# The last pair's second products one slot later, and the residual sum of an attention and expert kernel on VectorE

## The chip, the cores and the metric

The kernel runs on one core of one Trainium2 chip. The time is that of the device in microseconds (us), a median over runs; a profile of one execution lies beside it.

## The reference

The input x has 8 sequences of 512 rows of 256 floats. All of it is fp32, and the output has the shape of the input. `ln` is a layer norm over a row, without weights.

```python
x = x + ln(attn(ln(x)))          # 16 heads of 128 in 4 groups, causal; bias and position added to q and k
x = x + ln(moe(ln(x)))           # all rows as one batch

def attn(x):
    q = (x @ wq + bq) + pe ; k = (x @ wk + bk) + pe ; v = x @ wv + bv     # k, v: 4 groups of 4 heads
    return (softmax(causal(q @ k.T / sqrt(128))) @ v) @ wo

def moe(x):
    # softmax over 64 experts, best 6 of each row, at most 64 rows for an expert;
    # silu(x @ w_gate) * (x @ w_up) @ w_down for each, plus a shared expert of the same form
    ...
```

Note that `ln` does not change when a number is added to a whole row.

## The kernel before

**Slots.** The loop `for k in range(NK)` (line 1450) runs over 128 units: 8 sequences times 16 slots; a slot is one pair of row tiles and one group of heads. `b, s = divmod(k, NH)` are the sequence and the slot in it. The order of instructions on all engines is the order in which the loop's body calls its helpers (a manual schedule), so each engine has one queue, in that order. In each slot the unit k gets its scores (`scores`, psc on TensorE, reduced by VectorE, exponentials on ScalarE) and its weighing (`weigh`, reciprocal on VectorE, four TENSOR_SCALARs on GpSimd). In the next slot `turned` transposes 32x32 blocks on VectorE, sends them out to DRAM (`ex_d`, four DMAs on SyncE's queue) and reads them back as `et`. One slot later `mix` multiplies et by v (pav on TensorE, line 639), and ScalarE moves the result to `ao`.

**The projection in pairs.** For sequences 1 to 5 (`CROSSED`), the product with wo is done for two units at a time, a pair j. It has two parts. `straight` makes three products of ao (tile ps, bank o0), in the even slot. `cross` has GpSimd form four sums of ao (tile crossed), and `across` multiplies these (tile pc, bank o1). `add_up(j, 0)` and `add_up(j, 1)` add the banks to `partial`. For pairs 0 to 6 of a sequence, `across` and `add_up(j, 1)` stand in the odd slot. The last pair, n = 7, is due in slots 2 and 3 of the following sequence; before the change both of its parts stand in slot 2. `combine(b, 1)` on GpSimd then makes half of the rows o of the projection from partial (six instructions, lines 744 to 749).

**The feed-forward steps.** While sequence b + 1 runs, `feed_forward(b)` gives steps for sequence b, to be run at a place of a slot: `A` behind the weighing, `B` behind the projection's products, `M` behind the queries of later units, `D` at the slot's end. The steps that matter here, before the change:

| place | step | what it does |
|---|---|---|
| 2D | `copies` | combine(b, 1) |
| 3M | `scales(o)` | VectorE: statistics of o; GpSimd: rs_o, a power of -0.5 |
| 4A | `residual_sums` | normalizes o (sequences 1 to 4: VectorE makes shift_o, ScalarE does four ACTIVATEs; sequence 5: VectorE, four TENSOR_SCALARs), then GpSimd adds it to the rows xt, four TENSOR_TENSORs |
| 5M | `scales(xt)` | statistics of the new rows, rs_f on GpSimd |
| 5B | `store` | GpSimd's queue: DMA of xt, 512 KB, to x1_d |
| 6A | `rows` | normalizes the rows into xg (VectorE, and half of them ScalarE for sequences up to 4) |
| 6M | `turn` | VectorE transposes xg (into the buffer that o had), SyncE sends it out and reads it back (`exr_d`) |

**Buffers and queues.** The rows x of a sequence are in one of two buffers. The rows of the sequence after next are loaded by SyncE in slot 6 (`load_x`, line 187), behind that slot's et and once the store of x1 has read the buffer; their statistics (`st_a`) are taken by VectorE in slot 7. The tiles psc and third take turns in three PSUM banks, which VectorE frees.

Of the kernel before, what the change touches and what calls it, by code (L numbers as in the profile page):

```python
# [16 lines left out]
ALU = mybir.AluOpType  # L17
# [3 lines left out]
B, T, E = 8, 512, 256  # L21
NT = B * T
NI = T // P
# [21 lines left out]
CROSSED = range(1, EARLY + 1)  # L45

@with_exitstack
def sandwich_kernel(ctx, tc, x, wq, bq_t, wkv, bk_t, bv, wo, gate_wt, w_gate, w_up, w_down,
                    sh_gate_t, sh_up_t, sh_down_t, pe_t, out):
    nc = tc.nc  # L50
# [32 lines left out]
    def norm_scales(tiles, name, order=range(NI)):  # L83

        n = len(tiles)
        st = small.tile([P, n, 6], F32, tag="st", name=f"st_{name}")
        for i in order:
            nc.vector.bn_stats(st[:, i, :], tiles[i])
        return scales_of(st, n, name)
# [11 lines left out]
    def shifts(mv, rs, name):  # L101

        shift = small.tile([P, NI], F32, tag="shift", name=f"shift_{name}")
        nc.vector.scalar_tensor_tensor(shift, mv[:, :, 0], -1.0, rs, ALU.mult, ALU.mult)
        return shift

    def scale_on_act(dst, src, rs, shift, i):
        nc.scalar.activation(dst, src, AF.Identity, bias=shift[:, i : i + 1], scale=rs[:, i : i + 1])

    def tiles_of(t):  # L110
        return [t[:, i, :] for i in range(NI)]

    def rows_of(d, first):
        return d[first : first + T, :].rearrange("(i p) e -> p i e", p=P)

    def normalize(dst, src, mv, rs, i):
        nc.vector.tensor_scalar(dst, src, mv[:, i, 0:1], rs[:, i : i + 1], ALU.subtract, ALU.mult)

    def on_act(dst, src):
        nc.scalar.copy(dst, src)  # L120
# [35 lines left out]
    with ExitStack() as part:  # L156
# [497 lines left out]
        def tiles_at(j):  # L654

            return (1, 2) if j % 2 else (0, 3)

        def project(j, i):
            b, n = divmod(j, 2 * G)
            if n == 0 and i == 0:  # L660
                po[b] = [ps_o.tile([P, 2, E], F32, tag=f"o{n}", name=f"po_{b}_{n}") for n in range(2)]
            ao = results[j][:, tiles_at(j).index(i)]
            for h in range(QPG):
                nc.tensor.matmul(po[b][i // 2][:, i % 2, :], lhsT=ao[:, h, :], rhs=whole[j // 2][h],
                                 start=n == 0 and h == 0, stop=n // 2 == G - 1 and h == QPG - 1, skip_group_check=True)
# [46 lines left out]
        def multiply(j, factors, name, tag):  # L712
            bank_ = ps_o.tile([P, len(factors[0]), P], F32, tag=tag, name=f"{name}_{j}")
            for pair in range(2):
                for n, (a, w) in enumerate(factors[pair]):
                    nc.tensor.matmul(bank_[:, n, :], lhsT=a, rhs=w, start=pair == 0 and n == 0,  # L716
                                     stop=pair == 1 and n == len(factors[0]) - 1, skip_group_check=True)
            return bank_

        def straight(j):  # L720
            x11, x12, _, x22 = sides_of_results(j)
            w = sets[j // 2, 0]
            po[j, 0] = multiply(j, [[(x[:, n], w[k][:, n]) for k, x in enumerate((x11, x12, x22))] for n in range(2)],
                                "ps", "o0")

        def across(j):
            w, t = sets[j // 2, 1], crossed.pop(j)
            po[j, 1] = multiply(j, [[(t[:, k, n], w[k][:, n]) for k in range(4)] for n in range(2)], "pc", "o1")

        def add_up(j, part):  # L730
            b, n = divmod(j, 2 * G)
            sums, bank_ = partial[:, n % 2, (0, 3)[part] : (3, 7)[part], :], po.pop((j, part))
            if n < 2:
                on_act(sums, bank_)
            else:
                nc.vector.tensor_add(sums, bank_, sums)

        def combine(b, odd):

            t = partial[:, odd]  # L740
            if not odd:
                outs[b] = p1.tile([P, NI, E], F32, tag="xn", name=f"o_{b}")
            first, second = [outs[b][:, i, :].rearrange("p (u e) -> p u e", u=2) for i in tiles_at(odd)]
            nc.gpsimd.tensor_add(first[:, 0], t[:, 0], t[:, 1])
            nc.gpsimd.tensor_add(t[:, 5], t[:, 0], t[:, 5])
            nc.gpsimd.tensor_add(t[:, 6], t[:, 5], t[:, 6])
            nc.gpsimd.tensor_add(t[:, 3], t[:, 4], t[:, 3])
            nc.gpsimd.tensor_add(second, t[:, 2:5:2], t[:, 6:7].to_broadcast([P, 2, P]))
            nc.gpsimd.tensor_add(first[:, 1], t[:, 5], t[:, 3])

        def projected(k):

            j, odd = divmod(k, 2)
            j -= 2
            b, n = divmod(j, 2 * G)
            return j, odd, b, n, n == 2 * G - 1

        def projections(k):

            j, odd, b, n, last = projected(k)  # L760
            if j < 0:
                return
            if b not in CROSSED:
                for i in (() if odd else tiles_at(j)) if last else tiles_at(j)[odd : odd + 1]:
                    project(j, i)
            elif not odd:
                straight(j)
            elif not last:
                across(j)

        def projections_before(k):
# [4 lines left out]
        def projections_behind(k):  # L776
            j, odd, b, n, last = projected(k)
            if b in CROSSED:
                if not odd:
                    add_up(j, 0)  # L780
                elif not last:
                    add_up(j, 1)
                if last and not odd:
                    across(j)

        def projections_end(k):
            j, odd, b, n, last = projected(k)
            if b in CROSSED:
                if last and not odd:
                    add_up(j, 1)  # L790
                if n == 2 * G - 2 and odd:
                    combine(b, 0)

# [196 lines left out]
        def gate_up_hidden(key):  # L990
            l = pairs[key]
            pgu = l.pop("pgu")
            nc.vector.scalar_tensor_tensor(l["hid"], l["hid"], 1.0, pgu[:, 0, :], ALU.add, ALU.mult)
            nc.vector.scalar_tensor_tensor(l["hid"], l["hid"], 0.5, pgu[:, 1, :], ALU.mult, ALU.mult)
# [195 lines left out]
        def feed_forward(b):  # L1190


            xt, sums = seqs[b]["x"], po.pop(b, None)
            l = {}
# [10 lines left out]
            def scales(src, name):  # L1205
                l["scales"] = norm_scales(tiles_of(src), f"{name}{b}")

            def residual_sums():
# [7 lines left out]
                for i in range(NI):  # L1216
                    nc.gpsimd.tensor_add(xt[:, i, :], xt[:, i, :], l["o"][:, i, :])

            def store():
                nc.gpsimd.dma_start(out=rows_of(x1_d, b * T), in_=xt)  # L1220

            def rows():
                mv, rs = l.pop("scales")
                l["xg"] = p1.tile([P, NI, ROW], F32, tag="xg", name=f"xg_{b}")
                shift = shifts(mv, rs, f"f{b}") if b < EARLY else None
                for i in range(NI):
                    if b < EARLY and i % 2:
                        scale_on_act(l["xg"][:, i, :E], xt[:, i, :], rs, shift, i)
                    else:
                        normalize(l["xg"][:, i, :E], xt[:, i, :], mv, rs, i)  # L1230

            def turn():
                if b < EARLY - 1:
# [15 lines left out]
            def go(which, n=1):  # L1249
                return lambda: [next(l[which]) for _ in range(n)]  # L1250

            steps = {
                "2D": copies, "3M": lambda: scales(l["o"], "o"), "4A": residual_sums,
                "5M": lambda: scales(xt, "f"), "5B": store, "6A": rows,
                "6M": turn, "7A": shared_gate, "7B": go("f"), "8A": gate,
                "8D": go("r"), "9D": go("r"),
            }
            def choice_behind(steps):
                choose, then = steps.pop("8D"), steps.get("9A", lambda: None)
                return steps | {"9A": lambda: (choose(), then())}  # L1260

            if b == B - 2:
                steps["6D"] = steps.pop("6M")
            if b < B - 2:
                steps |= {"9A": go("f"), "9B": go("f"), "11A": go("f"), "11B": go("f")}
            if b < EARLY:
# [8 lines left out]
                steps = choice_behind(steps)  # L1275
# [15 lines left out]
            def down_late():  # L1291
# [3 lines left out]
            steps = choice_behind(steps) | {  # L1295
                "10A": go("r"), "10B": mark, "10D": gather_rows, "11D": lambda: gate_up("late"),
                "12A": lambda: gate_up_hidden("late"), "12D": lambda: turn_hidden("late"), "13A": down_late,
            }
# [151 lines left out]
        for k in range(NK):  # L1450
            b, s = divmod(k, NH)
# [86 lines left out]
            if s == 2 and b:  # L1538
                behind = feed_forward(b - 1)
# [34 lines left out]
        with tc.For_i(0, table["rest"], 1) as n:  # L1574
# [5 lines left out]
            for b in range(EARLY, B):  # L1580
                q, tag = [(p1, "hid"), (wpool, "e0"), (wpool, "e1")][b - EARLY]
                xg = q.tile([P, NI, LROW], F32, tag=tag, name=f"rest_xg_{b}")
# [75 lines left out]
```

## Time and profile before

| | us |
|---|---|
| median of three runs | 1350.15 (1346.76 to 1351.22) |
| the profiled execution | 1346.28 |
| its span, first to last instruction | 1344.6 |
| TensorE busy | 1319.8 |
| VectorE, GpSimd, ScalarE busy | 911.5, 660.3, 546.8 |

The granted clock of TensorE was 0.997 of full speed. The profile names engines PE (TensorE; PEld is its load of weights), DVE (VectorE), ACT (ScalarE), POOL (GpSimd), SP (SyncE); a q behind one is its queue. A group's row gives the source line, engine, operation, tiles written and read, shapes and count, then busy us, mean ns of one, idle time before it and what ended that. A timeline's row has the start, the time from first start to last end, the engine and line, and in brackets the idle time before it with what ended it. A row of the waits gives who waited for whom, us in total, times and the longest. A row of a tile gives the shortest, median and longest duration in ns. A row of windows has for each stretch the busy us of PE, PEld, DVE, ACT and POOL, the clock, the share of the 16 DMA engines and GB/s. An fp32 matmul is two records.

### The profile page before, as it was taken

The numbers are of one execution on the slowest core, as the hardware profiler recorded it, in microseconds if no ns is written. First come the engines' busy times: TensorE is split into PE (matmuls) and PEld (weight loads), VectorE is DVE, ScalarE is ACT, GpSimd is POOL, SyncE is SP. The second block draws the span as 40 slices with busy tenths as digits, with TensorE's granted clock in tenths as the row PEclk, the third lists the DMA queues.
The fourth block names the chain that finished last, engine by engine and source line by source line (L and its number), as shares of the span: only waits on it lengthen the run. The fifth ranks groups of instructions, "written<-read, shape, count | busy, mean of one in ns | idle before, by whom it ended". The sixth has DMA issues, their size and how long they took to land. (4 is left out here: it accounts for less than half of the span.)

```text
span 1344.6 us, 21778 instructions
## 1 busy us (share of the span) xinstructions
PE 1319.8 (98%) x6746; PEld 1018.7 (76%) x6746; DVE 911.5 (68%) x2931; ACT 546.8 (41%) x1665; POOL 660.3 (49%) x1080
## 2 busy tenths in 40 slices
PE   9999999999999999999999999999999999999997
PEld 7877887888778887788778877876667676767774
DVE  5575577777887678777886778666656444567645
ACT  3333354334443454344433443434343334444523
POOL 4556463436452563446434643355545444477711
PEclk9999999999999999999999999999999999999999
DMA  8676677756775676566765667579999889777712
GB/s 268 176 219 208 201 215 219 205 185 211 220 218 174 201 226 213 177 209 204 224 193 162 204 189 202 171 213 303 307 284 281 246 239 299 182 239 262 234 36 72
DMA packets 160435, 285.53 MB, mean 212 GB/s; under 512 B 17292, under 2 KB 123437, under 8 KB 160317
## 3 DMA queue, kind: packets, MB, share of 16 engines
q1 hardware_dynamic: 122893, 212.14, 52.6%
q0 software_dynamic: 13328, 36.05, 9.1%
q10 hardware_dynamic: 24096, 35.92, 8.5%
q8 instruction: 55, 0.90, 0.3%
q14 instruction: 63, 0.52, 0.1%
HBM read 168.44 MB, written 115.61 MB: 211 GB/s over the span
## 5 line engine op out<-in xcount | busy, mean ns | idle before, releaser
L584 POOL TENSOR_SCALAR e<-e,recip 128x512 f32<-128x512 f32 (+1 forms) x504 | 245.3, 525 | 424.1 <-DVE recip L580 367.7
L574 ACT ACTIVATE e<-e,least 128x32 f32<-128x32 f32 (+1 forms) x504 | 258.5, 514 | 260.4 <-DVE least L570 235.1
L639 PE MATMUL pav<-et,v 128*128 128x256 f32 x1280 | 300.4, 382 | 11.5 <-DMA et<-ex_d 8.9
L639 PEld LDWEIGHTS pav<-et,v 128*128 128x128 f32 x1280 | 241.5, 191 | 52.8 <-issue 7.1
L566 PE MATMUL psc<-kt,qt 128*128 128x32 f32 (+15 forms) x1024 | 274.9, 407 | 0.9 <-DVE qt L431 0.4
L570 DVE CUSTOM_DVE_ANT_0 e<-psc,mask 128x32 f32<-128x32 f32 (+1 forms) x504 | 204.2, 430 | 96.4 <-PE psc L566 93.8
L650 ACT ACTIVATE ao<-pav,bv_sb 128x256 f32<-128x256 f32 x255 | 107.1, 471 | 368.5 <-PE pav L639 344.7
L566 PEld LDWEIGHTS psc<-kt,qt 128*128 128x128 f32 x1024 | 161.5, 191 | 59.4 <-issue 25.9
L602 DVE STREAM_TRANSPOSE eb<-e 128x1024 f32<-128x1024 f32 (+1 forms) x252 | 197.5, 822 | 2.0 <-POOL e L584 1.5
L1021 POOL DMA_INDIRECT y_d<-dd,idx x32 | 51.1, 1597 | 93.2 <-ACT e L574 27.2
L574 ACT ACTIVATION_READ_ACCUMULATOR e<-e,least 128x1 f32 x504 | 94.6, 188 | 0.0
L716 PEld LDWEIGHTS pc<-set,crossed 128*128 128x128 f32 x640 | 77.0, 192 | 4.9 <-issue 1.7
L716 PE MATMUL pc<-set,crossed 128*128 128x128 f32 x640 | 78.8, 276 | 0.6 <-POOL crossed L710 0.6
L426 PE MATMUL pq<-xnt,wq_sb 128*128 128x256 f32 x320 | 75.5, 380 | 0.0
L716 PEld LDWEIGHTS ps<-set,ao 128*128 128x128 f32 x480 | 59.9, 192 | 15.3 <-issue 7.4
L470 PE MATMUL pq_back<-rows_joined,heads 128*128 128x256 f32 x264 | 71.3, 379 | 0.0
L388 PEld LDWEIGHTS pv<-wkv_sb,xnt 128*128 128x128 f32 x512 | 65.9, 192 | 4.5 <-issue 1.1
L388 PE MATMUL pv<-wkv_sb,xnt 128*128 128x128 f32 x512 | 67.5, 275 | 0.5 <-ACT ao L650 0.5
L426 PEld LDWEIGHTS pq<-xnt,wq_sb 128*128 128x128 f32 x320 | 59.2, 190 | 9.2 <-issue 0.7
L379 DVE SCALAR_TENSOR_TENSOR kt<-pk,bk_sb,pe_sb 128x512 f32<-128x512 f32 x32 | 24.0, 750 | 60.5 <-PE pk L377 58.5
L470 PEld LDWEIGHTS pq_back<-rows_joined,heads 128*128 128x128 f32 x264 | 50.2, 190 | 16.2 <-issue 8.2
L377 PE MATMUL pk<-xnt,wkv_sb 128*128 128x512 f32 x128 | 60.2, 593 | 0.3 <-ACT xnt L120 0.3
(281 smaller groups left out, 2017.6 us busy)
## 6 DMA issues: line engine op xcount, KB each, us to landing
ex_d<-eb SPq DMA_DIRECT2D x504, 160.0 KB
et<-ex_d SPq DMA_DIRECT2D x126, 640.0 KB
wgu<-in_w_gate ACTq DMA_DIRECT2D x32, 352.0 KB
wgu<-in_w_up ACTq DMA_DIRECT2D x32, 352.0 KB
wd<-in_w_down ACTq DMA_DIRECT2D x32, 352.0 KB
set<-wc_d SPq DMA_DIRECT2D x20, 512.0 KB
set<-ws_d SPq DMA_DIRECT2D x20, 384.0 KB
y<-y_d POOLq DMA_DIRECT2D x10, 512.0 KB, 6.8
```

The costliest lines, as they stand in the source:

```text
L377: nc.tensor.matmul(pk, lhsT=wkv_sb[:, c, g, 0, :], rhs=s["xnt"][:, c, :], start=c == 0, stop=c == NC - 1)
L388: nc.tensor.matmul(pv[:, i, :], lhsT=s["xnt"][:, c, ts(2 * n + i, P)], rhs=wkv_sb[:, c, g, 1, :], start=c == 0, stop=c == NC - 1, skip_gro ...
L426: nc.tensor.matmul(pq[:, n, :, :], lhsT=wq_sb[g][:, c, ts(2 * pair + n, D)], rhs=seqs[b]["xnt"][:, c, :].rearrange("p (u v) -> p u v", v=P ...
L470: nc.tensor.matmul(out, lhsT=factor[0], rhs=factor[1], start=first, stop=last, skip_group_check=True)
L566: nc.tensor.matmul(psc[:, :w], lhsT=halves[k // 2][:, at, :, :].rearrange("d h t -> d (h t)"), rhs=seqs[b]["kt"][g][:, :w], start=True, st ...
L570: nc.vector.tensor_tensor_reduce(out=e, in0=psc[:, :w].rearrange("p (c t) -> p c t", t=BS), in1=mask[:, T - w :].rearrange("p (c t) -> p c ...
L574: nc.scalar.activation(e, e, AF.Exp, bias=l["least"][:, q : q + 1], scale=-1.0, accum_out=l["total"][:, q : q + 1])
L584: engine.tensor_scalar(e, e, recip[:, q : q + 1], 1.0, ALU.mult, ALU.mult)
L602: nc.vector.transpose(eb[:, :, first : first + count, :, :].rearrange("p a j r t -> p j a r t"), weighed[k % 2][:, end - count : end, :, : ...
L639: nc.tensor.matmul(pav[n // NI][:, :, n % 2, :], lhsT=seqs[b]["v"][g][:, j, :], rhs=et[:, :, first + j, :], start=j == 0, stop=j == count ...
L650: nc.scalar.activation(ao, pav[n // NI][:, :, n % 2, :], AF.Identity, bias=bias)
L716: nc.tensor.matmul(bank_[:, n, :], lhsT=a, rhs=w, start=pair == 0 and n == 0, stop=pair == 1 and n == len(factors[0]) - 1, skip_group_chec ...
```

## The change

The last pair of a crossed sequence loses its exceptions: its `across` and `add_up(j, 1)` go to slot 3, as with all other pairs. For sequences 1 to 5 the steps behind are moved: combine to 3D, the statistics of o to 4A, the residual sum to 5A, the store to 5D. The sum is now made by VectorE in one instruction for each tile, o = o * rs + xt. This lacks -mean * rs, a number for each row (shift_o). The norm of the rows is taken from o as it is. The shift is added by GpSimd, xt = o + shift_o, just before the store, four TENSOR_SCALARs in place of four TENSOR_TENSORs.

```diff
             elif not odd:
                 straight(j)
-            elif not last:
+            else:
                 across(j)
...
                 if not odd:
                     add_up(j, 0)
-                elif not last:
+                else:
                     add_up(j, 1)
-                if last and not odd:
-                    across(j)
...
             if b in CROSSED:
-                if last and not odd:
-                    add_up(j, 1)
                 if n == 2 * G - 2 and odd:
                     combine(b, 0)
...
+            def residual_products():
+                mv, rs = l.pop("scales")
+                l["shift_o"] = shifts(mv, rs, f"o{b}")
+                for i in range(NI):
+                    nc.vector.scalar_tensor_tensor(l["o"][:, i, :], l["o"][:, i, :], rs[:, i : i + 1], xt[:, i, :],
+                                                   ALU.mult, ALU.add)
+
+            def shifted_store():
+                for i in range(NI):
+                    nc.gpsimd.tensor_scalar(xt[:, i, :], l["o"][:, i, :], l["shift_o"][:, i : i + 1], 1.0, ALU.add, ALU.mult)
+                store()
...
+                src = l["o"] if "shift_o" in l else xt
                 for i in range(NI):
                     if b < EARLY and i % 2:
-                        scale_on_act(l["xg"][:, i, :E], xt[:, i, :], rs, shift, i)
+                        scale_on_act(l["xg"][:, i, :E], src[:, i, :], rs, shift, i)
                     else:
-                        normalize(l["xg"][:, i, :E], xt[:, i, :], mv, rs, i)
+                        normalize(l["xg"][:, i, :E], src[:, i, :], mv, rs, i)
...
+            if b in CROSSED:
+                steps.pop("4A"), steps.pop("5B")
+                steps |= {"3D": steps.pop("2D"), "4A": steps.pop("3M"), "5A": residual_products,
+                          "5M": lambda: scales(l["o"], "f"), "5D": shifted_store}
```

## The prediction

> **What bounds the kernel now.** I read the page first, then TensorE's list of waits, then the timelines of TensorE, SyncE, VectorE and GpSimd around slots 4 to 8 of sequence 3, where the steps of sequence 2 run, and the DMA share by windows there. "Sequence 3, slot 4" is the slot that starts with the first psc of that unit (470.70 us; slots 5, 6, 7, 8 start at 478.72, 487.58, 495.69, 503.65).
>
> ```profile
> PE 1319.8 (98%) x6746; PEld 1018.7 (76%) x6746; DVE 911.5 (68%) x2931; ACT 546.8 (41%) x1665; POOL 660.3 (49%) x1080
> ...
> PE pav L639 <- DMA et<-ex_d: 8.9, 8, 2.8
> PE pav L639 <- DVE shift_o L104: 1.3, 3, 0.4
> PE pc L716 <- POOL crossed L710: 0.6, 1, 0.6
> ```
>
> TensorE is busy 98%: of 1344.6 us only 24.8 are idle, head and tail among them. The change takes no matmul away, so it can only remove waits, or make new ones. Waits near it are the last two rows and part of the first.
>
> ```profile
> 476.49 2.40 PE L639 MATMUL pav<-et,v 128*128 128x256 f32 x10 [0.45 <-DVE shift_o L104]
> ...
> 471.85 0.34 SPq L612 DMA_DIRECT2D et<-ex_d  x1
> ...
> 490.56 1.86 SPq L606 DMA_DIRECT2D ex_d<-eb  x4
> 494.91 0.34 SPq L612 DMA_DIRECT2D et<-ex_d  x1
> 495.41 0.40 SPq L187 DMA_DIRECT2D x<-in_x  x1
> ...
> 500.17 2.32 PE L639 MATMUL pav<-et,v 128*128 128x256 f32 x10
> ```
>
> The first row is the wait of slot 4. It is put down to VectorE's shift_o, but I take it for the transfer of et: that was issued 4.64 us earlier, and the same wait in sequences 2, 4 and 5 ends 4.50, 4.65 and 4.40 us after its et. So pav needs about 4.65 us from the issue of et. In slot 7 it has 5.26 us (500.17 - 494.91): 0.61 us to spare. SyncE's queue is in order: that et waits for the landing of ex_d, and the load of x stands behind it.
>
> ```profile
> 483.87 1.40 DVE L88 BATCH_NORM_STATS2 st_f<-x 128x6 f32<-128x256 f32 x4
> 485.19 0.36 DVE L94 BATCH_NORM_AGGREGATE mv_f<-st_f 128x2 f32<-128x6 f32 x4
> 485.58 0.40 DVE L96 TENSOR_SCALAR ve_f<-mv_f 128x4 f32<-128x4 f32 x1
> 487.78 0.75 DVE L379 SCALAR_TENSOR_TENSOR kt<-pk,bk_sb,pe_sb 128x512 f32<-128x512 f32 x1 [1.79 <-PE pk L377]
> ...
> 501.30 1.41 DVE L88 BATCH_NORM_STATS2 st_a<-x 128x6 f32<-128x256 f32 x4 [0.91 <-DMA x<-in_x]
> ...
> 485.21 0.81 POOL L1220 DMA_DIRECT2D x_d<-x  x1
> 486.08 1.03 POOL L98 TENSOR_TENSOR rs_f<-ve_f,mhalf 128x4 f32<-128x4 f32 x1
> ```
>
> In slot 5 VectorE has 1.79 us idle before kt; from kt to the end of slot 6 it has next to none. GpSimd issues the store of the sums before rs_f. In slot 7 VectorE already waits 0.91 us for x.
>
> **Part by part.** *Second products to slot 3.* 16 matmul records (1.79 us of TensorE's order) leave slot 2 and enter slot 3: same work, two slots of about 8 us in place of 9.90 and 6.18. Slot 3 being longer, TensorE reaches slot 4's pav 1.8 us later after the transposes that feed et. Gain: the waits of sequences 2 to 5, 0.29 + 0.45 + 0.44 + 0.14 = 1.32 us. If another cause stood behind shift_o it would be 0. In slot 3, pav of the unit before comes 1.8 us later in its slot, and its slot starts as much earlier: no change. In sequence 6 the products wait 0.61 us for GpSimd's crossed; half a turn later that is made: -0.61 us, or 0 if the slot waits elsewhere.
>
> *Steps half a slot later.* combine is six GpSimd instructions of about 3 us behind slot 3's weighing; they end some 1.7 us into slot 4, before VectorE's reciprocal there (476.28 - 470.70 = 5.6 us in), behind which 4A's statistics (1.4 + 0.36 + 0.17 = 1.9 us) now stand. VectorE was idle 2.22 us at the end of slot 4, so they fit; queued behind them is only ask_sum, whose reader is in slot 5. Cost 0. The add_up of part 1 moves too: 0.68 us of VectorE in slot 3, where the statistics of o leave 1.9.
>
> *Sum by VectorE.* ScalarE loses 4 x 0.586 us for blocks 1 to 4 and GpSimd 4 x 0.728 us, neither on TensorE's path: 0. VectorE gains, in slot 5, shift_o (0.09) and four products of 128x256 with two SBUF inputs. The nearest rows:
>
> ```profile
> L1399 DVE SCALAR_TENSOR_TENSOR x<-y,rs_y,x x4: 480/480/485, 1339.8 to 1340.9; 128x256 f32<-128x256 f32 x4
> ...
> L117 DVE TENSOR_SCALAR o<-o,mv_o,rs_o x8: 381/575/801, 924.8 to 1176.7; 128x256 f32<-128x256 f32 x8
> ```
>
> L1399 is the same form with GpSimd idle, one each 0.40 us. Four of L117 beside GpSimd's weighing took 2.09 us (0.52 each; alone their median on x is 0.40). The new four run beside slot 5's weighing. At 0.40 they need 1.69 us of the 1.79: hidden, with 0.10 left. I take 0.50, nearer to the row with the same neighbour: 2.09 us, 0.30 over. What is late then is kt, and behind it the reductions of slot 6. The eight psc matmuls took 2.16 us in slot 6 and 2.00 in slot 7, so they already follow VectorE there; I let the 0.30 through in four sequences: +1.2 us (0 at 0.40; 6.0 at 0.80).
>
> By the Trainium skill, "GPSIMD Engine Reference", section "Key points", GpSimd shares its SBUF interfaces with VectorE and contends with instructions that have two SBUF inputs. That speaks against the change: this trace has no such pair, L117 being the other kind that the page names. Were the page wrong for these, the term would be 0 and the sum 1.2 us less.
>
> *Shift at the store.* rs_f now waits for VectorE until about 487.7 (485.98 + 1.7) where it began at 486.08. Behind it on GpSimd: four TENSOR_SCALARs (0.467 apart as L1338, 1.9 us), the store's issue (0.81), four crossed (2.9) and slot 6's weighing. So: rs_f to 488.8, store issued at 490.7 in place of 485.21, crossed done at 494.4, weighing from there (before: 493.31) to 496.4. Its reader is slot 7's transpose at 497.05, and ScalarE's next ao needs crossed's inputs free by 495.1: both just hold, cost 0. The store is another matter.
>
> ```profile
> 487.00:488.00 1.00, 1.00 (x5) 0.61 (x4) 0.22 (x1) 0.00 (x0) 0.92 (x3) 1.00 1.09 352
> ...
> 491.00:492.00 1.00, 1.00 (x7) 0.87 (x6) 0.85 (x4) 1.00 (x3) 0.00 (x0) 1.00 0.62 125
> 492.00:493.00 1.00, 1.00 (x6) 0.90 (x5) 1.00 (x3) 0.27 (x2) 0.00 (x0) 1.00 0.96 182
> ```
>
> Before, it had the DMA engines to itself (352 GB/s, last columns DMA share and GB/s). Issued at 490.7 it starts some 1.4 us later, amid ex_d, which holds them at a share of 0.96. 512 KB at 352 GB/s is 1.5 us; by so much ex_d lands later, hence et, x and what follows on SyncE. Bounds: 0 if it slips between, 2.9 at the 182 GB/s of ex_d. I take 1.5. Slot 7's pav has 0.61 to spare: +0.88 each in sequences 2, 3 and 4, +2.6 us (0 to 6.9). Sequence 5's slots 6 and 7 are longer (8.99 and 12.16) and cover it. x lands 1.5 later; VectorE's tail of slot 7, which ended 503.58, ends 505.07, and slot 8 starts 0.88 later, at 504.53: the first reduction comes 0.54 into it in place of 0.43, +0.1 each, +0.3 (0 to 4). The store itself lands in about 4 us, before SyncE reaches x.
>
> *Sum*: -1.32 - 0.61 + 1.2 + 2.6 + 0.3 = +2.2 us. The profiled execution took 1346.28 (span 1344.6), 3.9 under the median of the three runs, so 1348.5 there; from the median 1350.15, **1352.3**.
>
> **Rivals.** *Quiet case*: store and products hidden, only the first two terms act: -1.9, 1348.2. For: DMA is free from 494.5 to 496. Against: the share of 0.96 where the store goes.
>
> *Slower*: VectorE overruns slot 5. At 0.80 per product (the longest L117) the overrun is 4 x 0.80 + 0.09 - 1.79 = 1.5 us, 6.0 over four sequences in place of 1.2: +7.0, 1357.2. It decides from 0.61 per product on, where the whole sum passes +4. For: the 0.10 us left in slot 5. Against: other instructions with an SBUF and a PSUM input keep 0.48 beside the weighing.
>
> *Faster*: nothing is added, and in sequence 6 the waits for et in slots 4 and 5 (1.80 and 1.00) go as slot 3 grows: -1.9 - 2.8 = -4.7, 1345.4. Against: these transfers queue behind weight loads, which the change doesn't touch.
>
> **How the numbers follow.** Forecast 0.33, with its own range 1350 to 1354; quiet 0.15; slower 0.35; faster 0.15; 0.02 left. About 0.3% (4 us) is what can be told from no change here; the three runs spread 4.5. Forecast and quiet lie within it: 0.48. Faster 0.16 with a little of what is left, slower 0.36. The range leaves out a tenth at each end: 1345.5 to 1358.
>
> **What would show it.** Right: slots 2 and 3 near 8 us; no wait at pav in slot 4; a new wait for et at slot 7's pav of 0.5 to 1.3 us in sequences 2 to 4, its et issued about 1.5 later; the four products at 0.4 to 0.6 apart. Wrong: products at 0.8, kt late by a microsecond; or no wait in slot 7; or SyncE standing at the load of x for the store.

## The result, and the profile after

Over eight runs each, measured side by side, the changed kernel takes 1351.46 us (1349.18 to 1354.14) and the kernel before 1347.11 (1345.42 to 1351.22): a ratio of 1.0028, with a 95% interval of 1.0014 to 1.0041. It is slightly slower, within the 0.3% that the prediction set as its bound. The profiled execution after took 1349.18 us (span 1347.5), 2.90 more than the one before.

The page's busy times and TensorE's list of waits, after:

```profile
PE 1320.5 (98%) x6746; PEld 1018.3 (76%) x6746; DVE 921.4 (68%) x2948; ACT 538.5 (40%) x1649; POOL 659.6 (49%) x1080
...
PE pav L639 <- DMA et<-ex_d: 11.5, 12, 2.4
PE psc L566 <- DVE qt L505: 2.0, 3, 0.8
...
PE pav L639 <- DVE shift_o L104: 0.4, 1, 0.4
```

ScalarE lost 8.3 us, VectorE gained 9.9, TensorE has the same work. Among the waits, shift_o has nearly gone and the wait for crossed is gone; but pav waits longer for et, and a row that the prediction did not have is new in this size: psc waits for VectorE's qt (0.3 us before, 2.0 now). To place them I cut the span at the first psc of each unit:

| slot (sequences 2, 3, 4) | before | after |
|---|---|---|
| 2 | 9.90, 9.90, 9.90 | 8.11, 8.11, 8.11 |
| 3 | 6.18, 6.18, 6.18 | 7.97, 7.97, 7.97 |
| 4 | 7.87, 8.02, 8.02 | 7.34, 7.34, 7.34 |
| 5 | 8.85, 8.85, 8.85 | 8.85, 8.85, 9.00 |
| 6 | 8.11, 8.11, 8.11 | 8.11, 8.11, 8.11 |
| 7 | 7.97, 7.97, 7.99 | **10.45, 10.34, 10.33** |

Sequences 2 to 5 together: 585.9 us before, 590.2 after. Slot 4 gives 2.26 back (0.53 + 0.68 + 0.68, and 0.37 in sequence 5); slot 7 costs 7.19; slots 2 and 3 cancel. What else differs by more than 0.1 us is slot 5 of sequence 4 (0.15 longer) and slots 0 and 15 of sequence 2 (0.56 and 0.38 shorter: the execution before had waits of 0.60 and 0.14 us for et there, which come and go between executions). Sequence 6 is 3.1 us shorter and sequence 7, up to its last matmul, 1.5 longer, but these two, where experts' weights are loaded, differ that much between executions: sequence 7 took 217 to 224 us over the profiles of this study, the run of 1461 us below left out. The sums over sequences 2 to 5 are the steadier measure, and I use them below.

The wait of slot 4 in sequence 3 is gone; its pav and the group ahead of it now:

```profile
476.76 0.38 PE L470 MATMUL pq_back<-rows_joined,heads 128*128 128x256 f32 x1
476.98 2.32 PE L639 MATMUL pav<-et,v 128*128 128x256 f32 x10
```

SyncE's queue and GpSimd around slots 6 and 7 of sequence 3. In the changed kernel slots 5 to 8 start at 479.14, 487.99, 496.10 and 506.44 us.

```profile
490.97 2.05 SPq L606 DMA_DIRECT2D ex_d<-eb  x4
497.48 0.34 SPq L612 DMA_DIRECT2D et<-ex_d  x1
497.92 0.40 SPq L187 DMA_DIRECT2D x<-in_x  x1
```

```profile
483.79 2.75 POOL L584 TENSOR_SCALAR e<-e,recip 128x448 f32<-128x448 f32 x4 [3.26 <-DVE recip L580]
488.25 1.02 POOL L98 TENSOR_TENSOR rs_f<-ve_f,mhalf 128x4 f32<-128x4 f32 x1 [1.71 <-DVE ve_f L96]
489.26 1.84 POOL L1224 TENSOR_SCALAR x<-o,shift_o 128x256 f32<-128x256 f32 x4
491.40 0.82 POOL L1228 DMA_DIRECT2D x_d<-x  x1 [0.30 <-POOL x L1224]
```

The store is issued 3.41 us into slot 6 (before: 2.37 ahead of it), 0.43 behind ex_d's first issue. et follows at 9.49 us from slot 6's start, 2.16 later than the 7.33 before, and x at 9.93 instead of 7.84. The DMA share and rate from 491.99 on (last two columns):

```profile
491.99:492.99 1.00, 1.00 (x6) 0.90 (x5) 0.85 (x3) 0.69 (x3) 0.96 (x2) 1.00 1.01 200
492.99:493.99 1.00, 1.00 (x7) 0.87 (x6) 1.00 (x5) 0.15 (x1) 0.93 (x2) 1.00 0.93 210
493.99:494.99 1.00, 1.00 (x6) 0.88 (x5) 1.00 (x2) 1.00 (x3) 1.00 (x2) 1.00 0.97 293
494.99:495.99 1.00, 1.00 (x9) 0.97 (x8) 1.00 (x4) 0.81 (x3) 1.00 (x3) 1.00 1.02 257
```

The engines are all but full for four microseconds, at a mean of 240 GB/s. From the first to the last packet of the store (493.57 to 496.41) their time divides into its queue, q0, and SyncE's, q1:

```profile
q0 software_dynamic: 141, 0.52, 61.8%
q1 hardware_dynamic: 200, 0.23, 36.8%
```

Now TensorE and VectorE in slots 5 to 8, the same sequence:

```profile
501.95 2.40 PE L639 MATMUL pav<-et,v 128*128 128x256 f32 x10 [1.12 <-DMA et<-ex_d]
504.18 0.59 PE L470 MATMUL pq_back<-rows_joined,wq_sb 128*128 128x256 f32 x2
504.62 1.05 PE L388 MATMUL pv<-wkv_sb,xnt 128*128 128x128 f32 x8
506.44 2.38 PE L566 MATMUL psc<-kt,qt 128*128 128x32 f32 x8 [0.77 <-DVE qt L505]
```

```profile
483.66 2.32 DVE L1219 SCALAR_TENSOR_TENSOR o<-o,rs_o,x 128x256 f32<-128x256 f32 x4
485.90 0.47 DVE L505 SCALAR_TENSOR_TENSOR qt<-third,bq_sb,ht 128x256 f32<-128x256 f32 x1
...
488.19 0.75 DVE L379 SCALAR_TENSOR_TENSOR kt<-pk,bk_sb,pe_sb 128x512 f32<-128x512 f32 x1
...
504.11 1.41 DVE L88 BATCH_NORM_STATS2 st_a<-x 128x6 f32<-128x256 f32 x4 [3.19 <-DMA x<-in_x]
...
505.91 0.47 DVE L505 SCALAR_TENSOR_TENSOR qt<-third,bq_sb,ht 128x256 f32<-128x256 f32 x1
```

Two waits stand in slot 7. pav waits 1.12 us for et. And VectorE stands 3.19 us at st_a for x; behind the statistics on its queue is qt<-third, the one that frees a PSUM bank, so the psc that opens slot 8 waits 0.77 us for it. VectorE's kt starts 0.20 us into slot 6, exactly as before.

### The profile page after: what moved, and what is told of

It reads as the page before. It is cut to its first block, busy times and chain, and to the rows that moved or that the text cites. A ratio compares the mean times of both kernels' runs of the same rounds, so it can differ in the third digit from the quotient of the medians.

```text
span 1347.5 us, 21762 instructions
## 1 busy us (share of the span) xinstructions
PE 1320.5 (98%) x6746; PEld 1018.3 (76%) x6746; DVE 921.4 (68%) x2948; ACT 538.5 (40%) x1649; POOL 659.6 (49%) x1080
## 5 line engine op out<-in xcount | busy, mean ns | idle before, releaser
L639 PEld LDWEIGHTS pav<-et,v 128*128 128x128 f32 x1280 | 241.8, 191 | 53.5 <-issue 7.6
```

What stands on the lines that cost most here:

```text
L639: nc.tensor.matmul(pav[n // NI][:, :, n % 2, :], lhsT=seqs[b]["v"][g][:, j, :], rhs=et[:, :, first + j, :], start=j == 0, stop=j == count ...
```

## The experiments

Theory **T**: the store's place in time makes all of the loss; its packets share the DMA engines with ex_d, and et and x, behind ex_d on SyncE's queue, are late. Rival **C**: VectorE's and GpSimd's added work in slots 5 and 6 makes it. All kernels but one in one table; the ratio is to the kernel before, measured beside each, and the last two columns are of one profiled execution of each.

| kernel | ratio, 95% interval | sequences 2 to 5, us | slot 7 in sequences 2, 3, 4 |
|---|---|---|---|
| before | 1 | 585.9 | 7.97, 7.97, 7.99 |
| changed | 1.0028 [1.0014, 1.0041] | 590.2 | 10.45, 10.34, 10.33 |
| changed, measured again | 1.0022 [1.0005, 1.0038] | 590.0 | 10.45, 10.17, 9.69 |
| shift and store in slot 5 | 0.9984 [0.9965, 1.0003] | 585.2 | 8.73, 7.97, 8.10 |
| the same, again | 0.9986 [0.9970, 1.0001] | 584.5 | 7.97, 8.04, 8.26 |
| before, store at 2.1 us of slot 6 | 1.0021 [0.9999, 1.0042] | 589.3 | 8.96, 9.35, 8.70 |
| before, store at 3.2 us of slot 6 | 1.0052 [1.0034, 1.0069] | 593.3 | 10.15, 10.42, 10.55 |
| changed, old rows stored in slot 5, additions to a spare buffer | 0.9982 [0.9966, 0.9998] | 583.9 | 8.13, 7.97, 8.01 |
| changed, half the store late | 0.9995 [0.9977, 1.0013] | 587.2 | 9.05, 8.98, 8.76 |
| changed, statistics of x in slot 8 | 1.0015 [1.0003, 1.0028] | 588.6 | 9.45, 9.46, 9.21 |
| sum on VectorE alone | 1.0010 [0.9992, 1.0027] | 586.1 | 7.97, 8.05, 8.29 |
| products in slot 3 alone | 1.0003 [0.9986, 1.0019] | 588.5 | 7.97, 8.26, 7.97 |
| changed, a fifth product | 1.0035 [1.0020, 1.0050] | 592.7 | 10.62, 10.47, 10.39 |

**The store back to slot 5.** The shift additions and the store move half a slot ahead; all else stays.

```diff
-                          "5M": lambda: scales(l["o"], "f"), "5D": shifted_store}
+                          "5M": lambda: scales(l["o"], "f"), "5B": shifted_store}
```

> The changed kernel with one step moved: the four additions of the shift and the store stand at 5B, behind slot 5's weighing, so on GpSimd they go ahead of rs_f. Theory T (the store's transfer runs amid the ex_d writes of slot 6, so et and x come late): the store is issued about 0.5 us into slot 6 and is through before ex_d starts at 3.6; slots 7 of sequences 2 to 4 go from 10.4 back to 8.0, the time to about 1344.5, ratio to the kernel before 0.998. Rival C (VectorE and GpSimd hinder one another where the products run beside the weighing, and the transposes of the rows come late for that): nothing of this changes, slots 7 stay at 10.4, time about 1351, ratio 1.003.

> The changed kernel with the shift additions and the store half a slot earlier, in slot 5 behind the weighing (first run: 0.9984 [0.9965, 1.0003] of the kernel before, slot 7 at 8.0 to 8.7). Theory T: again about 5 us under the changed kernel in the same call, 1 to 4 under the kernel before: ratio 0.997 to 0.9995. Rival Q (slots 4 and 7 only trade their waits, nothing is left): ratio 0.9995 to 1.001.

> The changed kernel itself, beside the others on the same chip. Both theories: ratio 1.001 to 1.004 to the kernel before; it gives the difference to the version with the store in slot 5 (T: 4 to 6 us).

SyncE's queue and TensorE of this kernel, first run, sequence 3 (slots 6, 7 and 8 start at 487.61, 495.72 and 503.68):

```profile
490.58 1.89 SPq L606 DMA_DIRECT2D ex_d<-eb  x4
494.96 0.34 SPq L612 DMA_DIRECT2D et<-ex_d  x1
495.39 0.40 SPq L187 DMA_DIRECT2D x<-in_x  x1
```

```profile
500.20 2.32 PE L639 MATMUL pav<-et,v 128*128 128x256 f32 x10
...
503.68 2.32 PE L566 MATMUL psc<-kt,qt 128*128 128x32 f32 x8
```

The store is issued 0.42 us into slot 6, et at 7.35 as in the kernel before, and both waits of slot 7 are gone. Beside each other, this version takes 1347.38 us and the changed kernel 1352.01: 4.6 less. All the added work is still there, so C is wrong for most of the loss. Against the kernel before it comes out at 0.9984 and 0.9986, and each interval just includes 1: a version that beats both is likely, not shown. In two of its six slots 7 st_a still starts later than before, and they take 8.73 and 8.26; why stays open.

**The store alone, moved in the kernel before.** In the steps of sequences 1 to 3 only.

```diff
+            if b in (1, 2, 3):
+                steps["6P"] = steps.pop("5B")
...
             projections_before(k)
+            side(s, "P")
```

> The kernel before with one step moved: in sequences 2 to 4 the store of the sums stands behind the four crossed of slot 6 on GpSimd, issued about 2.5 us into that slot; the work on VectorE, ScalarE and TensorE is that of before. T: slots 7 of sequences 2 to 4 go from 8.0 to about 10.3, the time to 1353 or 1354, ratio 1.005. C: no product runs beside a weighing, so slots 7 stay at 8.0 and the time at 1347, ratio 1.000.

Here the expectation was too long: 8.7 to 9.35 instead of 10.3. But the store was issued at 2.10 us, earlier than the 3.41 of the changed kernel, and et came only 1.15 late. Three TENSOR_SCALARs of GpSimd on dead rows, put ahead of the same store, bring it to 3.2:

```diff
...
+                    for i in range(3):
+                        nc.gpsimd.tensor_scalar(l["o"][:, i, :], l["o"][:, i, :], 1.0, 1.0, ALU.mult, ALU.mult)
+                    sums_store()
```

> The kernel before, in the steps of sequences 1 to 3 alone the store of the sums stands in slot 6 behind the projection's products, and GpSimd first does three TENSOR_SCALARs of 128x256 on the dead rows o (about 0.47 us each), so that the store is issued at about 3.4 us into slot 6, where the changed kernel issues it (2.1 in the run with the store alone moved). Theory T (the store's packets share the DMA engines with slot 6's ex_d; et and the load of x behind it on SyncE's queue come late by that, and slot 7's products and slot 8's reductions wait): et is issued about 9.4 us after slot 6's start, and slot 7 lasts about 10.3 us in sequences 2 to 4 (8.0 before, 8.7 to 9.35 with the store at 2.1); the whole is 4 to 7 us over the kernel before, ratio 1.003 to 1.005. Rival C (the remaining length of slot 7 in the changed kernel comes from VectorE's and GpSimd's added work in slots 5 and 6, not from the time of the store): slot 7 stays at 8.7 to 9.4, ratio at most 1.0025.

GpSimd, SyncE and TensorE of this kernel, sequence 3 (slots 6, 7, 8 at 491.09, 499.21, 509.62):

```profile
493.23 1.15 POOL L1267 TENSOR_SCALAR o<-o 128x256 f32<-128x256 f32 x3
494.32 0.81 POOL L1220 DMA_DIRECT2D x_d<-x  x1
```

```profile
494.07 2.13 SPq L606 DMA_DIRECT2D ex_d<-eb  x4
500.64 0.34 SPq L612 DMA_DIRECT2D et<-ex_d  x1
```

```profile
504.88 2.40 PE L639 MATMUL pav<-et,v 128*128 128x256 f32 x10 [1.02 <-DMA et<-ex_d]
...
509.62 2.38 PE L566 MATMUL psc<-kt,qt 128*128 128x32 f32 x8 [1.03 <-DVE qt L505]
```

Both waits of the changed kernel are back, in their size, with nothing else of the change in it: et 9.55 us from slot 6's start, slot 7 at 10.42. One microsecond in the store's issue, 2.1 to 3.2, made slot 7 another 1.1 to 1.9 us longer.

**The changed kernel with the old rows stored in slot 5.** Both forms leave the attention's part out of the rows that are stored, so they serve to measure the place of the store and nothing else. The first form added the shift to o in place.

```diff
-                    nc.gpsimd.tensor_scalar(xt[:, i, :], l["o"][:, i, :], l["shift_o"][:, i : i + 1], 1.0, ALU.add, ALU.mult)
-                store()
+                    nc.gpsimd.tensor_scalar(l["o"][:, i, :], l["o"][:, i, :], l["shift_o"][:, i : i + 1], 1.0, ALU.add, ALU.mult)
...
+                          "5B": store, "5M": lambda: scales(l["o"], "f"), "5D": shifted_store}
```

> The changed kernel, but what is stored is the rows before the sum, at 5B, and the four additions of the shift at 5D go into o and are not stored (the stored residual is left without the attention's part). All engines' work and their order stay; only the 512 KB move to the start of slot 6. T: slots 7 of sequences 2 to 4 at 8.0, time about 1344.5, ratio 0.998. C: slots 7 at 10.4, ratio 1.003.

This missed as a measurement of the whole: 1461.38 us, a ratio of 1.084. o then holds shifted rows while its mean is that of the unshifted ones, so the router gets other rows, and the loop for rows that found no place in an expert runs at the end: 183 us follow the start of the last unit's scores where the changed kernel has 68. Up to there it can be compared: sequences 2 to 5 take 584.0 us. With the additions written to a spare buffer instead:

> The changed kernel, but the store keeps its old place in slot 5 and sends the rows without the sum, and GpSimd's four shift additions stay where the change put them and write to a spare buffer. The sum is thereby missing from the rows that the end adds up; all work but the place of the store's issue is that of the changed kernel. Theory T: slots 2 to 6 as in the changed kernel (8.11, 7.97, 7.34, 8.85, 8.11), slot 7 back at 8.0 in sequences 2 to 4 with no wait for et at its pav; 5 to 7 us under the changed kernel, 1.995 to 0.999 of that being a ratio of 0.996 to 0.999 to the kernel before. Rival C (the added work on VectorE and GpSimd makes weighing and the transposes of xg late, and these hold SyncE's queue): slot 7 stays above 9 us, ratio 1.001 to 1.003.

583.9 us and a ratio of 0.9982. All additions stand at their late place on GpSimd, and slot 7 is back at 8.0. For slot 7 only the place of the DMA counts.

**Half the store late.** Two of four row tiles are sent in slot 5 as old rows, two behind the additions.

```diff
...
+            def half_store(half):
+                two = slice(2 * half, 2 * half + 2)
+                nc.gpsimd.dma_start(out=rows_of(x1_d, b * T)[:, two, :], in_=xt[:, two, :])
...
```

> The changed kernel with a store of half the size at its place: 256 KB (two of four row tiles) are sent in slot 6 behind the shift additions, the other 256 KB in slot 5 behind the weighing, as old rows; the additions for those two tiles write to a spare buffer, so the sum is missing in half of the rows that the end adds up. Theory T, by amount (the delay of et is the time that the store's packets take from ex_d): et is issued at about 8.4 us into slot 6 (9.49 with 512 KB, 7.33 with none), slot 7 lasts 8.7 to 9.3 us in sequences 2 to 4, the whole is 3 to 5 us under the changed kernel, ratio 0.999 to 1.001. Rival A (the fact of a transfer on GpSimd's queue at that moment costs, not its amount): slot 7 stays at 10.0 to 10.4, ratio 1.002 to 1.004.

et was issued at 8.37, 8.06 and 8.08 us (none late: 7.33; 512 KB: 9.49), slot 7 took 8.76 to 9.05. Amount counts, not the fact. (These halves were issued at 3.11, 2.75 and 2.84 us, a little earlier than the whole store; but 512 KB issued at 2.10 already put et at 8.48, so the earlier issue alone does not make the difference.) What was not expected is which wait remained:

```profile
501.67 2.32 PE L639 MATMUL pav<-et,v 128*128 128x256 f32 x10
...
506.17 2.38 PE L566 MATMUL psc<-kt,qt 128*128 128x32 f32 x8 [0.85 <-DVE qt L505]
```

pav no longer waits for et at all in this slot (0.20 us in sequence 2, nothing in 4); the whole microsecond is psc's wait for VectorE, hence for x. (The profiled execution, 1354.59 us against a median of 1351.45, also had a wait of 2.81 us at pav in slot 3 of sequence 6.)

**Which of the two transfers sets slot 7.** Over all these kernels slot 7 lasts as long as the start of st_a in it plus 2.33 us, or 7.97: 8.12 + 2.33 = 10.45, 7.36 + 2.33 = 9.69, 6.65 + 2.33 = 8.98, 6.40 + 2.33 = 8.73. So x, not et, seemed to set the end. To part them, st_a goes to slot 8:

```diff
-            if b <= EARLY and s == 7:
+            if b <= EARLY and s == (8 if b in (2, 3, 4) else 7):
```

> The changed kernel with VectorE's statistics of the new rows x (st_a) one slot later, in slot 8 instead of 7, in sequences 2 to 4. The store stays late, so et and x are late as in the changed kernel. It is to tell which of the two late transfers sets slot 7. In every run so far slot 7 lasts as long as the start of st_a in it plus 2.33 us, or 7.97. Theory X (x sets it: VectorE stands at st_a for x, the read of third behind it frees the PSUM bank late, and slot 8's psc waits; the wait of pav for et lies inside this): slot 7 falls to what et alone asks, pav's start at 5.85 to 6.26 us and 3.48 behind it, 9.3 to 9.75 us in place of 10.33 to 10.45, with no wait of psc for VectorE in slot 8. Rival E (et sets it): slot 7 stays at 10.2 to 10.5. Slot 8 has to take 1.9 us more of VectorE's work and the wait for the square root of it on GpSimd, and may grow by 0 to 2 us, so the whole time decides nothing: ratio 1.000 to 1.004.

TensorE, sequence 3 (slot 7 starts at 496.00):

```profile
501.91 2.40 PE L639 MATMUL pav<-et,v 128*128 128x256 f32 x10 [1.19 <-DMA et<-ex_d]
...
505.46 2.27 PE L566 MATMUL psc<-kt,qt 128*128 128x32 f32 x8
```

pav still waits as long, psc no longer does, and slot 7 ends at 9.46: 9.45, 9.46 and 9.21, where theory X has 9.3 to 9.75. Late et alone is worth 1.2 to 1.5 us for each sequence; late x brings it to 2.3 to 2.5, with the wait for et inside. The slot's end follows x.

**The other parts.** Sum on VectorE with the products still in slot 2 (the lines of the first hunks of the change are those of before again):

```diff
...
-                steps |= {"3D": steps.pop("2D"), "4A": steps.pop("3M"), "5A": residual_products,
-                          "5M": lambda: scales(l["o"], "f"), "5D": shifted_store}
+                steps |= {"4A": residual_products, "5M": lambda: scales(l["o"], "f"), "5B": shifted_store}
```

> Only the second part of the change: the sum by VectorE and the shift at the store, in the places that the steps had before (products at 4A, shift and store at 5B); the last pair's products stay in slot 2. T: the store is issued near the end of slot 5, slots 7 stay at 8.0, the wait of slot 4 stays too; time within 2 us of 1347, ratio 0.999 to 1.001. C: the products now run beside the weighing of slot 4 and cost there what they cost in slot 5; slot 7 or slot 5 longer by one to two us in four sequences, ratio 1.003 or more.

Slot 4 keeps its waits (7.91, 8.07, 7.94), slot 7 is at 8.0 to 8.3: the sum on VectorE brings nothing that can be told by itself, and the moved products are what takes slot 4 to 7.34. The other way round, products in slot 3 with the sum left to ScalarE and GpSimd:

```diff
-                steps |= {"3D": steps.pop("2D"), "4A": steps.pop("3M"), "5A": residual_products,
-                          "5M": lambda: scales(l["o"], "f"), "5D": shifted_store}
+                steps |= {"3D": steps.pop("2D"), "4A": steps.pop("3M"), "5A": residual_sums,
+                          "5B": store}
```

> The first and second part of the change alone: second products of the last pair in slot 3 and the steps half a slot later, but the sum stays ScalarE's and GpSimd's, as before (eight instructions), in slot 5, with the store behind it. What the sum on VectorE is for: if the sum stays on GpSimd (weighing 1.9 us, then four sums of 0.73), VectorE's statistics of the new rows wait for it until about 0.5 us into slot 6, and kt stands behind them. Theory: slots 2, 3 and 4 as in the changed kernel (8.11, 7.97, 7.34); kt 1.2 to 2 us late in sequences 1 to 4, slot 5 and 6 together 1 to 2 us longer; slot 7 at 8 to 9 us; in all 3 to 8 us over the version with the store in slot 5, ratio 1.001 to 1.005. Rival: kt's delay is taken up elsewhere and the sum may stay where it was: ratio 0.998 to 0.9995.

VectorE, sequence 3 (slot 6 starts at 488.50):

```profile
486.93 0.43 DVE L88 BATCH_NORM_STATS2 st_f<-x 128x6 f32<-128x256 f32 x1 [2.05 <-POOL x L1213]
...
488.98 0.43 DVE L88 BATCH_NORM_STATS2 st_f<-x 128x6 f32<-128x256 f32 x1 [0.26 <-POOL x L1213]
...
489.80 0.74 DVE L379 SCALAR_TENSOR_TENSOR kt<-pk,bk_sb,pe_sb 128x512 f32<-128x512 f32 x1
```

VectorE now stands 2.05 us for GpSimd's sum, kt is 1.1 us late, and slot 6 takes 9.22, 9.21 and 8.91 us in place of 8.11. Half a slot later the sum no longer fits on GpSimd; made by VectorE, which had the room, it leaves kt and slot 6 where they were. How much room, a fifth product shows:

```diff
...
+                nc.vector.scalar_tensor_tensor(spare_rows[:, 0, :E], l["o"][:, 0, :], rs[:, 0:1], xt[:, 0, :],
+                                               ALU.mult, ALU.add)
```

> The changed kernel with a fifth product of the same form behind the four in VectorE's slot 5 of sequences 1 to 5, written to a spare buffer (0.58 us each in the changed kernel). There the four fill VectorE's idle time to 0.03 us. Theory F (full: whatever comes on top reaches kt and lengthens the slots): kt starts about 0.55 us later in slot 6, slots 5 and 6 together grow by 0.4 to 0.6 us in each of sequences 1 to 4, together 2 us over the changed kernel; sequence 5 hides it. Rival S (there is still room, as kt's late start is taken up by slack in TensorE's queue): slots 5 and 6 stay at 16.96 together, nothing in the time.

It took 0.59 us, and slots 5 and 6 together grew from 16.96, 16.96 and 17.11 to 17.35, 17.35 and 17.48. Only sequence 2 shows it cleanly: kt starts 0.39 us later there and slot 6 alone is 0.38 longer. In sequences 3 and 4 all or most of the growth stands in slot 5, at a pav whose et was issued late, as told below. In the changed kernel kt had 0.03 us of idle time ahead of it in sequences 2, 3 and 5: the four fill the room to its edge.

## Why the prediction was right, point by point

The forecast of "no difference that can be told" was right, and 1352.3 stands 0.8 us from the measured 1351.46. Its sum was not: the terms erred both ways, and the base was 3.0 us too high (the median of three runs, 1350.15, against 1347.11 of eight), which hid that the change cost 4.35 between medians instead of 2.2. That the number came so near is luck.

- *Slot 4's waits, -1.32.* The mechanism is right: moved products alone take them away. The size is 2.26. The row's idle time is not the whole price of a wait. Without one, pav starts 0.16 us before the end of the group ahead (476.98 against 476.76 + 0.38); with one that is lost, and pav's row takes 2.40 us in place of 2.32. A wait of 0.45 cost 0.68.
- *Sequence 6, -0.61.* Slots 2 and 3 together gave 0.88 here and in five more of the ten profiles with the products in slot 3; in the other four, slot 3 was 0.1 to 4.7 us longer. Slots 4 to 6 came out between 44.9 and 48.2 us with the products in slot 3 and between 46.0 and 47.2 without. The whole of sequence 6 took 239.2 to 240.3 us in seven of the ten and 242.1 to 246.3 in the other three, against 241.8 to 242.6 in the four without: a gain there is likely and not shown, and what the rival "faster" hoped for stays open.
- *VectorE's overrun, +1.2.* Measured: none. kt starts 0.20 us into slot 6 in each of sequences 2 to 5. The products took 0.58 each, nearer the rival's 0.61 than the 0.50 taken. What failed is the room: the prediction counted the 1.79 us ahead of kt; there was also the 0.20 that qt<-third had waited for TensorE (first row below, before), and ve_f, which had stood beside GpSimd's issue of the store, fell from 0.40 to 0.17. Together 2.22, and 4 products with shift_o filled all but 0.03. The rule of the Trainium skill that was weighed, "GPSIMD Engine Reference", section "Key points", that GpSimd contends with VectorE's instructions with two SBUF inputs, agrees with this case: 0.58 beside weighing against 0.40 of the same form alone, and the four weighing instructions took 2.75 us instead of 1.89 (second row, before).

```profile
483.47 0.48 DVE L505 SCALAR_TENSOR_TENSOR qt<-third,bq_sb,ht 128x256 f32<-128x256 f32 x1 [0.20 <-PE third L470]
...
483.37 1.89 POOL L584 TENSOR_SCALAR e<-e,recip 128x448 f32<-128x448 f32 x4 [2.19 <-DVE recip L580]
```

- *A term that the prediction does not have.* Slot 5 of sequence 4 is 0.15 us longer (0.30 when measured again), and this is not VectorE: it stood idle ahead of kt there, and with the products moved and no sum on VectorE the same slot took 9.15. Its et was issued 0.73 us into the slot instead of 0.65 ahead of it, and pav came late:

```profile
627.93 0.34 SPq L612 DMA_DIRECT2D et<-ex_d  x1
...
631.79 2.43 PE L639 MATMUL pav<-et,v 128*128 128x256 f32 x10
...
636.40 0.75 DVE L379 SCALAR_TENSOR_TENSOR kt<-pk,bk_sb,pe_sb 128x512 f32<-128x512 f32 x1 [0.18 <-PE pk L377]
```

In the ten profiles with the products in slot 3, et was late in this way in 16 of the 30 slots 5 of sequences 2 to 4, which cost 0.15 to 0.52 us each, and in none of 12 with them in slot 2. In each of the 16, and in none of the other 14, a packet of the queue that the profile's page calls "instruction" (q8, 16 KB) fell amid ex_d's packets. One of the 12 had such a packet too, nearer to ex_d's end, and its et was on time. That the packet makes ex_d late is argued from this alone; no run changes it.

- *GpSimd's chain in slot 6, cost 0.* Right: crossed ended 0.4 us later in its slot than forecast, and no row of the waits names it.
- *The store, +2.6.* The mechanism is right, and was named with its place: a late store, ex_d, et, a wait at slot 7's pav. The delay of et was 2.16 instead of 1.5. The prediction priced 512 KB at 352 GB/s, the rate of the store by itself, though it goes out amid ex_d's packets: at the mean 240 GB/s of the windows above it would be 2.2 us, an estimate made after the result, which fits (for half the store it gives 1.1, and et was 0.7 to 1.0 late). The store's own packets took 61.8% of 2.84 us, 1.76 us of all engines; where the other 0.4 of the delay comes from is not shown.
- *x and slot 8, +0.3.* This is the step that failed. The prediction saw that x lands late and that VectorE's tail moves with it, then let slot 8 begin regardless and asked only when its first reduction could start. But that tail holds the read of third, which frees a bank for psc. Before, the tail ended 0.07 us ahead of slot 8 (503.58 against 503.65; 0.27 in sequence 2, 0.05 in 4), and after, with psc waiting for it, 0.05: there was next to no slack. Store and x together cost 7.19, not 2.9. The two rows of before:

```profile
503.10 0.48 DVE L505 SCALAR_TENSOR_TENSOR qt<-third,bq_sb,ht 128x256 f32<-128x256 f32 x1
503.65 2.36 PE L566 MATMUL psc<-kt,qt 128*128 128x32 f32 x8
```

- *What would show it.* Slots 2 and 3 near 8, no wait in slot 4, the new wait for et and the products' pace are there. The wait was 1.1 to 1.6 us, above the 0.5 to 1.3 for one sequence, and et 2.2 late instead of 1.5.

## What to carry to other kernels

When a transfer is moved, price its bytes at the rate that the windows show where it will land, not where it was (here 2.2 us by that estimate, 1.5 by the other, 2.16 measured), and follow every transfer queued behind those it delays, each to its own reader. The reader to look for is an in-order engine that stands at the late data with the release of someone else's buffer behind it: its slack is the distance from the end of its tail to the next user of that buffer, and here that was 0.07 us in the sequence shown. An edit can gain and lose in the same sequence; cut the span at a fixed instruction of each unit and compare slot by slot, since a whole time of +0.3% hid -2.3 and +7.2.

## What the runs showed of the hardware that was not expected

VectorE's four SCALAR_TENSOR_TENSORs of 128x256 fp32 with two SBUF inputs took 0.58 us each in the mean beside GpSimd's TENSOR_SCALARs (0.40 alone), and slowed these from a mean of 0.47 to 0.69: both sides lose some 45%. The loss is uneven: the four took 0.48 to 0.83 us (0.48 each alone, where the next starts 0.08 before the end), and GpSimd's four, of different widths, 0.34 to 1.17 (0.35 to 0.64 with the sum left to GpSimd). VectorE's two TENSOR_SCALARs on xg, with one such input, took 1.01 us together beside weighing and 1.63 beside crossed, GpSimd's TENSOR_TENSORs, which themselves took 0.73 to 0.78. A store of 512 KB on GpSimd's queue landed 5.4 us after its issue when it fell amid ex_d's packets (4.1 before, both medians over the profile).
